# Attention with a quantized feed-forward block: reordering the first and last attention steps, rotated sums kept in PSUM, and a rotation table laid out by rows

## The chip, the cores and the metric

The kernel runs on one core of a Trainium2 chip. The metric is the device time of one execution in microseconds (us). Five engines work side by side, each through its own queue in order: TensorE (PE: matmuls and transposes, results into PSUM), VectorE (DVE), ScalarE (ACT), GpSimd (POOL) and SyncE (SP, which issues most of the DMA transfers here). Engines wait for each other through semaphores. [...] SBUF is the working memory.

## What is computed

One transformer layer, for 8 batches of 128 rows and 512 columns. The first half is a cross-attention with 32 query heads and 8 key/value heads of 128 columns, the second a gated feed-forward block whose weights are rounded to a table of 16 values (NF4) in blocks of 64. The reference, cut:

```python
def attention(query, key, value, mask, Wq, Wk, Wv, Wo):   # query = layernorm(x)
    q = apply_rope((query @ Wq).reshape(b, t, 32, 128))
    k = apply_rope((key @ Wk).reshape(b, t, 8, 128))
    v = (value @ Wv).reshape(b, t, 8, 128)
    logits = einsum('btkgd,bTkd->bkgtT', q, k) * ATTN_MULT
    logits = 30.0 * tanh(logits / 30.0)
    weights = softmax(where(mask, logits, -1e30))
    return einsum('bkgtT,bTkd->btkgd', weights, v).reshape(b, t, 4096) @ Wo

def apply_rope(x):      # x * cos + rotate_half(x) * sin
    ...

def ffn(x, w1, w2, w3):
    dq1, dq2, dq3 = nf4(w1), nf4(w2), nf4(w3)
    return (silu(x @ dq1.T) * (x @ dq2.T)) @ dq3.T

x = x + attention(layernorm(x), ctx, ctx, mask, Wq, Wk, Wv, Wo)
x = x + ffn(layernorm(x), w1, w2, w3)
```

## The kernel before

The order of every engine's work is written out by hand: the program is built in that order, each engine runs its own part of it as a queue, and no scheduler moves anything.

**Matrix products.** Each float32 operand is split in a high part (a copy to a narrower float, ScalarE, L155) and a low part (the difference, L156, VectorE or GpSimd). `product` (L165) does three matmuls for each pair of operands: high times low (L169), high times high (L170), low times high (L171).

**Stage 1, keys and values** (to about 106 us): the context is loaded in eight tiles, keys `pk` and values `pvp` are computed in tiles of 128 x 512 and written to DRAM. `loads` (L585) is the order of the loads on SP's queue: the first key weight, four context tiles, the table of rotations `tab`, two more key weights, and the rest. `rope` (L454) rotates a key or query tile: ScalarE copies the two halves of the PSUM tile, exchanged, into `rs` (L461, L462); VectorE multiplies the PSUM tile with the cosines into `rc` (L463); GpSimd multiplies `rs` with the signed sines (L464); and a sum of both goes to `kr` or `qr` (L465, on GpSimd unless an engine is named). `rc` and `rs` have two buffers each.

**Stage 2, attention** (to about 600 us): 64 steps `i` (the loop at L759), each for one batch and one key/value head with its four query heads. In step `i` stand, in this order: query tiles of the next half (`q_proj`, four in each group of four steps; the first group has them at steps 0, 0, 1 and 2), `project(i - 3)` (the output projection `po`, and the sum into `acc`, L702), `turn(i - 2)` (transposes `pt_a` and the split into `aT`), `values(i - 1)` (`pv`, and its division by the row sums into `ad`), and `scores(i)` (`pl`, then tanh and exp on ScalarE at L678 and L679, then the mask on GpSimd at L681). Query tiles `pq` and transposes `pt_a` share two PSUM banks with the tag `q`; `pl` has one bank (`s`), `po` one (`wo`). Near the end the sums of the second layer norm are taken from `acc` (`LayerNorm.sums`, L131: statistics at L133 and L134), its rows `xn_y` follow (L150), and their transposes `pt_y`, which use the banks `q`, `s` and `wo`.

**Dequantization** runs beside all that as a stream: one unit is a bound on ScalarE (`nm_w`, L195) and an accumulation on VectorE in PSUM (`nc_w`, L201), of 1024 columns in most tiles. `pump(n)` (L404) puts `n` units into the queues where it is called; `store` splits a finished tile, and for the first two weights writes it to DRAM. The last weight's tiles `w3t` stay in SBUF.

**Stage 3, feed-forward** (from about 603 us): `gate_up` for two halves and eleven tiles of hidden columns, then the down projection `pd` (from L865) with splits `hs` of the hidden values; the tiles `w3t` are dequantized while it begins, the last one (96 rows) only shortly before it is used.

Of the kernel before, what the change touches and what calls it, by code (L numbers as in the profile page):

```python
# [11 lines left out]
F32 = mybir.dt.float32  # L12
# [8 lines left out]
P = 128  # L21
B, T, D = 8, 128, 512
# [3 lines left out]
KT = D // P  # L26
# [19 lines left out]
def tables():  # L46
    e = np.arange(0, HD, 2, dtype=np.float32)
    inv = (np.float32(1.0) / np.float32(10000.0) ** (e / np.float32(HD))).astype(np.float32)
    phase = np.arange(T, dtype=np.float32)[:, None] * inv[None, :]
    phase = np.tile(phase, (1, 2)).T  # L50
    cos, sin = np.cos(phase).astype(np.float32), np.sin(phase).astype(np.float32)
    sgn = sin.copy()
    sgn[:HD // 2] *= -1


    bias = np.array([np.nextafter(BOUNDS[i], np.float32(np.inf)) if i in NEG else -BOUNDS[i]
                     for i in range(15)] + [0], dtype=np.float32) * np.float32(BIG)
    return (np.ascontiguousarray(np.stack([cos, sgn])),
            np.ascontiguousarray(np.broadcast_to(bias, (P, 16))))


# [1 line left out]
def block_kernel(ctx: ExitStack, tc: tile.TileContext, x, ctxt, mask, wq, wk, wv, wo, w1, w2, w3, w12t, w3_t,  # L63
                 rope_tab, nf_bias, out):
    nc = tc.nc
    V, S, Q, E = nc.vector, nc.scalar, nc.gpsimd, nc.tensor
# [4 lines left out]
    tp = ctx.enter_context(tc.tile_pool(name="tp", bufs=2))  # L71
# [20 lines left out]
    tab = cp.tile([P, 2, T], F32, name="tab")  # L92
# [69 lines left out]
            E.transpose(pt[:, k * P:(k + 1) * P], src[:, k * P:(k + 1) * P], ident)  # L162
        return lambda: split(hi, lo, pt.rearrange("p (k t) -> p k t", k=KT), V)

    def product(out, pairs, start=True, stop=True):  # L165

        n = len(pairs)
        for i, ((ah, al), (bh, bl)) in enumerate(pairs):
            E.matmul(out, ah, bl, start=start and i == 0, stop=False)  # L169
            E.matmul(out, ah, bh, start=False, stop=False)  # L170
            E.matmul(out, al, bh, start=False, stop=stop and i == n - 1)  # L171


    def scales(a, r, w):
# [115 lines left out]
    class Scales:  # L290
# [23 lines left out]
        def turn(self, tag):  # L314
            pt = bank(tag, f"pt_ar_{self.h}")[:2 * 16, :P]
            E.transpose(pt, self.s.rearrange("p t b -> p (t b)"), ident)

            def later():
                t = nf.tile([2 * 16, P], F32, tag="nf_st", name=f"art_{self.h}", bufs=1)
                S.copy(t, pt)  # L320
                nc.sync.dma_start(scale_d.rearrange("t j b h -> (t j b) h")[:, self.h * P:(self.h + 1) * P], t)
            stored.append(later)
# [81 lines left out]
    def pump(n):  # L404

        credit[0] += n
        while credit[0] > 0:
            credit[0] -= next(stream, n + credit[0])
# [17 lines left out]
    with ExitStack() as c1:  # L426

        xT = [wide(f"xT_{i}") for i in range(2)]
        cosq = a1.tile([P, T], F32, name="cosq")
        sgnq = a1.tile([P, T], F32, name="sgnq")  # L430
        mt = a1.tile([P, T], F32, name="mt")
        qr = {}
# [18 lines left out]
            t = wp.tile([P, 2, KT, HD], F32R, tag="wq", name=name, bufs=6)  # L451
            return t, lambda: split(t[:, 0], t[:, 1], raw, V if name == "wk_0" else Q)

        def rope(dst, src, cos, sgn, name, engine=None):  # L454

            hd = HD // 2
            every = lambda ap: ap.unsqueeze(1).to_broadcast([P, 4, T])
            src4 = src.rearrange("p (b t) -> p b t", t=T)
            c = tp.tile([P, 4, T], F32, tag="t1", name=f"rc_{name}")
            s = tp.tile([P, 4, T], F32, tag="t2", name=f"rs_{name}")  # L460
            S.copy(s[:hd], src4[hd:])  # L461
            S.copy(s[hd:], src4[:hd])  # L462
            V.tensor_tensor(c, src4, every(cos), ALU.mult)  # L463
            Q.tensor_tensor(s, s, every(sgn), ALU.mult)  # L464
            return lambda: (engine or Q).tensor_tensor(dst, c, s, ALU.add)  # L465
# [6 lines left out]
        def q_proj(u, g):  # L472
            kv, half = divmod(u, 2)
            if g == 0:
                qr[u] = a1.tile([P, 4, G, T], F32, tag="qr", name=f"qr_{u}", bufs=2)
            pq = bank("q", f"pq_{u}_{g}")
            w, t = wqt[kv, g], xT[half]
            product(pq, [((w[:, 0, k], w[:, 1, k]), (t[:, 0, k], t[:, 1, k])) for k in range(KT)])
            return lambda: rope(qr[u][:, :, g, :], pq, cosq, sgnq, f"q{u}_{g}", V if u < 1 else None)


        with ExitStack() as c3:
# [28 lines left out]
            def k_proj(kv, half):  # L511
                cols = slice(half * 512, half * 512 + 512)
                pk = bank("q", f"pk_{kv}_{half}")
                w = wkt[kv]
                product(pk, [((w[:, 0, k], w[:, 1, k]), (cT[0][:, k, cols], cT[1][:, k, cols])) for k in range(KT)])

                def later():
                    kr = kv1.tile([P, 512], F32, tag="kr", name=f"kr_{kv}_{half}")
                    add = rope(kr.rearrange("p (b t) -> p b t", t=T), pk, tab[:, 0], tab[:, 1], f"k{kv}_{half}",
                               V if kv < 3 else Q)  # L520

                    def last():
                        add()
                        nc.sync.dma_start(kr_d[kv, half], kr)
                    return last
                return later
# [51 lines left out]


            def load_tab(*_):  # L580
                nc.sync.dma_start(tab, rope_tab.rearrange("c d t -> d c t"))
                return lambda: None

            load = {"t": load_tab, "k": load_k, "c": load_c, "v": load_v, "q": load_first_q}
            loads = [(-1, "k", 0, 0)] + [(-1, "c", 0, k) for k in range(KT)]  # L585
            loads += [(-1, "t", 0, 0), (-1, "k", 1, 0), (0, "k", 2, 0), (0, "c", 1, 0), (0, "c", 1, 1), (1, "c", 1, 2), (1, "c", 1, 3)]
            loads += [(2, "v", 0, 0), (2, "v", 0, 1), (3, "v", 0, 2), (3, "v", 0, 3), (5, "k", 3, 0), (9, "k", 4, 0)]
            loads += [(12, "k", 5, 0), (15, "k", 6, 0), (17, "v", 1, 0), (18, "v", 1, 1), (19, "k", 7, 0)]
            loads += [(20, "v", 1, 2), (21, "v", 1, 3)] + [(24 + 2 * g, "q", g, 0) for g in range(G)]
# [82 lines left out]
        def scores(i):  # L672
            u, kv, b, bb = where(i)
            pl = bank("s", f"pl_{i}")
            E.matmul(pl, krt[kv, u % 2][:, bb * T:(bb + 1) * T], qr[u][:, bb].rearrange("p g t -> p (g t)"),  # L675
                     start=True, stop=True)
            th = at.tile([P, 512], F32, tag="th", name=f"th_{i}", bufs=3)
            S.activation(th, pl, AF.Tanh, scale=ATTN_MULT / CAP)  # L678
            S.activation(th, th, AF.Exp, scale=CAP)  # L679
            em[i] = th.rearrange("p (g t) -> p g t", g=G)  # L680
            Q.tensor_tensor(em[i], em[i], mt.unsqueeze(1).to_broadcast([P, G, T]), ALU.mult)  # L681
# [15 lines left out]
        def project(i):  # L697
            u, kv, b, bb = where(i)
            po = bank("wo", f"po_{i}")
            product(po, [((aT[i][:, 0, g], aT[i][:, 1, g]), (wot[kv, g][:, 0], wot[kv, g][:, 1]))  # L700
                         for g in range(G)])
            V.tensor_tensor(acc[b], acc[b], po, ALU.add)  # L702
# [46 lines left out]
                V.tensor_tensor(hT[half, h // 4][:, h % 4], sg, pu, ALU.mult)  # L749
            return later  # L750

        due = {0: [("o", 0, 0)], 1: [("o", 0, 1), ("o", 0, 2), ("o", 0, 3)]}
        xn = {}

        def turned(ks, tags):
# [3 lines left out]
        for i in range(N):  # L759
            u, kv, b, bb = where(i)  # L760
            s8 = i % 8
            if kv + 1 < NKV:
                if s8 == 0:
                    load_kv(kv + 1)
                if s8 < 4:
                    load_q(kv + 1, s8)
                else:
                    load_o(kv + 1, s8 - 4)
                due.setdefault(i + (2 if i < 4 else 1), []).append(("q" if s8 < 4 else "o", kv + 1, s8 % 4))
            tiles = {0: (0, 1), 1: (2,), 2: (3,), 3: ()}.get(i, (bb,)) if u + 1 < 2 * NKV else ()  # L770
            later = [q_proj(u + 1, g) for g in tiles]
            later = [f() for f in later]
            if i > 1:
                store()
                end_store()
            pump(1.5 if 2 < i < 58 else 1 if i in (0, 1, 58, 59) else 0)
            if 0 <= i - 3:
                project(i - 3)
            if i in (59, 61):
                ln = LayerNorm((i - 59, i - 58), f"y{i - 59}")  # L780
            if 59 <= i < 63:
                ln.sums(i - 59)
            if 0 <= i - 2:
                turn(i - 2)
            if 0 <= i - 1:
                values(i - 1)
            scores(i)
            if i == 61:
                xn.update({k: pair.rows(k, "xn") for k in (0, 1)})
            for f in later:  # L790
                f()
            pump(1.65 if 2 < i < 58 else 2 if i == 58 else 0)
            if i == 62:
                turned((0, 1), "qq")
            if i in (60, 62):
                ln.finish(Q)
                pair = ln
            for k in due.pop(i, ()):
                todo[k]()
            if i >= 61:  # L800
                load_w12(i - 61)

        project(N - 3)
        xn.update({k: pair.rows(k, "t2") for k in (2, 3)})
        turned((2,), "s")
        turn(N - 2)
        values(N - 1)
        turned((3,), "s")
        ln = LayerNorm((4, 5), "y1")
        ln.sums(4)  # L810
# [113 lines left out]
```

## Time and profile before

| what | us |
|---|---|
| median of three runs | 794.67 (794.63 to 794.92) |
| the profiled execution | 793.06 |
| its span, first to last instruction | 791.3 |
| TensorE busy | 777.4 (98% of the span) |
| VectorE busy | 626.9 (79%) |
| ScalarE busy | 586.0 (74%) |
| GpSimd busy | 472.6 (60%) |

The busy times are of the profiled execution. A matmul's end in the profile is modelled, and matmuls overlap, so the space between the starts of two matmuls tells more than the length of one. In a line of the timeline the first number is the start in us from the start of the span, the second the length; then engine, source line, operation, output and inputs, shape, how many were merged (x), and in brackets how long the engine stood idle before it and what ended that. In the waits view a line names the waiting engine, tile and line, what it waited for, then the sum in us, the number of waits and the longest.

### The profile page before, as it was taken

How to read it: one execution, taken by the hardware profiler on the slowest of the kernel's cores; microseconds unless marked ns; L12 is line 12 of the kernel's file. 1: busy time of each engine (PE TensorE's matmuls, PEld its weight loads, DVE VectorE, ACT ScalarE, POOL GpSimd, SP SyncE). 2: the span in 40 equal slices, each digit the busy share in tenths (PEclk: the TensorE clock that was granted, in tenths of full speed). 3: DMA queues.
4: the chain of work that ended last, by engine and by line, in shares of the span. 5: the costliest groups of instructions: out<-in, count | busy, mean ns of one | idle time of the engine just before them, and what ended most of it. 6: DMA issues, size and time to landing. Idle time of an engine off the chain costs nothing.

```text
span 791.3 us, 11200 instructions
## 1 busy us (share of the span) xinstructions
PE 777.4 (98%) x3737; PEld 628.3 (79%) x3737; DVE 626.9 (79%) x836; ACT 586.0 (74%) x821; POOL 472.6 (60%) x415
## 2 busy tenths in 40 slices
PE   8999997999999999999999999999999999999998
PEld 7788875778777878878787887878777888888887
DVE  6767677788888887888888878888876688888981
ACT  7458667889796978879797979898732587779740
POOL 3568448688787878777797877878652122232110
PEclk9999999999999999999999999999999999999999
DMA  6966735525337434517336432414133163651011
GB/s 229 297 190 198 213 107 174 147 80 173 90 120 206 136 104 121 173 55 227 94 109 191 133 92 94 138 57 128 58 104 107 49 173 98 186 160 47 11 53 54
DMA packets 73457, 102.44 MB, mean 129 GB/s; under 512 B 7832, under 2 KB 42968, under 8 KB 73400
## 3 DMA queue, kind: packets, MB, share of 16 engines
q1 hardware_dynamic: 70232, 90.19, 37.9%
q0 software_dynamic: 3168, 11.54, 4.6%
q8 instruction: 30, 0.49, 0.3%
q14 instruction: 27, 0.22, 0.1%
HBM read 79.32 MB, written 22.38 MB: 129 GB/s over the span
## 4 chain that ended last, share of the span: by engine, by line
PE 93%; ACT 2%; DVE 2%; issue 1%; DMA 1%; SPq 0%; POOL 0%; DVEq 0%; POOLq 0%; ACTq 0%
PE po L171 7%; PE po L170 7%; PE po L169 7%; PE pq L171 7%; PE pq L169 7%; PE pq L170 7%; PE pv L688 7%; PE pl L675 7%; PE pt_a L162 3%; PE pd L170 3%; PE pd L169 3%; PE pd L171 3%; PE pu L171 3%; PE pg L171 3%; PE pg L170 3%; PE pu L170 3%
## 5 line engine op out<-in xcount | busy, mean ns | idle before, releaser
L201 DVE SCALAR_TENSOR_TENSOR nc_w<-nm_w,nc_w 128x1024 f32<-128x1024 bf16 (+1 forms) x238 | 284.6, 1196 | 62.1 <-ACT nm_w L195 51.4
L195 ACT ACTIVATE nm_w<-w_w,bias 128x1024 bf16<-128x1024 f32 (+1 forms) x255 | 275.9, 1115 | 18.3 <-POOL w_w L205 8.7
L681 POOL TENSOR_TENSOR th<-th,mt 128x512 f32<-128x512 f32 x64 | 83.4, 1303 | 88.4 <-ACT th L679 81.5
L169 PE MATMUL pq<-xT,wq 128*128 128x512 f32 x256 | 123.9, 484 | 0.0
L169 PE MATMUL po<-wo,aT 128*128 128x512 f32 x256 | 102.1, 399 | 1.1 <-DVE acc L702 0.6
L171 PE MATMUL po<-wo,aT 128*128 128x512 f32 x256 | 100.5, 393 | 2.6 <-DVE aT L156 2.6
L171 PE MATMUL pq<-xT,wq 128*128 128x512 f32 x256 | 100.4, 392 | 0.0
L170 PE MATMUL pq<-xT,wq 128*128 128x512 f32 x256 | 100.1, 391 | 0.0
L170 PE MATMUL po<-wo,aT 128*128 128x512 f32 x256 | 100.0, 391 | 0.0
L464 POOL TENSOR_TENSOR rs_q<-rs_q,sgnq 128x512 f32<-128x512 f32 x64 | 83.0, 1296 | 13.0 <-ACT rs_q L462 12.9
L465 POOL TENSOR_TENSOR qr<-rc_q,rs_q 128x512 f32<-128x512 f32 x60 | 78.5, 1308 | 0.0
L678 ACT ACTIVATE th<-pl 128x512 f32<-128x512 f32 x64 | 38.3, 598 | 49.7 <-PE pl L675 48.4
L688 PE MATMUL pv<-vt,th 128*128 128x129 f32 x512 | 67.8, 275 | 1.3 <-POOL th L681 1.3
L169 PEld LDWEIGHTS pq<-xT,wq 128*128 128x128 f32 x256 | 48.2, 188 | 22.5 <-issue 10.8
L170 PEld LDWEIGHTS pq<-xT,wq 128*128 128x128 f32 x256 | 48.2, 188 | 22.3 <-issue 13.9
L675 PE MATMUL pl<-qr,krt 128*128 128x512 f32 x128 | 65.5, 593 | 0.0
L688 PEld LDWEIGHTS pv<-vt,th 128*128 128x128 f32 x512 | 62.2, 192 | 1.7 <-POOL th L681 1.7
L463 DVE TENSOR_TENSOR rc_q<-pq,cosq 128x512 f32<-128x512 f32 x64 | 44.0, 687 | 20.0 <-ACT rs_q L462 17.3
L205 POOL TENSOR_TENSOR w_w<-w_w,s_w 128x1024 f32<-128x1024 f32 (+1 forms) x17 | 39.6, 2327 | 33.1 <-DMA s_w<-scale_d 32.5
L171 PEld LDWEIGHTS po<-wo,aT 128*128 128x128 f32 x256 | 48.0, 188 | 14.1 <-DVE aT L156 3.8
L169 PEld LDWEIGHTS po<-wo,aT 128*128 128x128 f32 x256 | 48.1, 188 | 14.0 <-issue 2.1
L171 PEld LDWEIGHTS pq<-xT,wq 128*128 128x128 f32 x256 | 48.0, 188 | 10.7
(145 smaller groups left out, 1692.0 us busy)
## 6 DMA issues: line engine op xcount, KB each, us to landing
w12t_d<-dqt SPq DMA_DIRECT2D x22, 512.0 KB
w<-w12t_d POOLq DMA_DIRECT2D x22, 512.0 KB, 4.5
s_w<-scale_d SPq DMA_DIRECT2D x40, 256.0 KB
raw_wq<-in_L_xattn_Wq SPq DMA_DIRECT2D x32, 256.0 KB
raw_wo<-in_L_xattn_Wo SPq DMA_DIRECT2D x32, 256.0 KB
s_w<-scale_d SPq DMA_DIRECT2D x86, 64.0 KB
ws<-in_L_ffn_w SPq DMA_DIRECT2D x20, 256.0 KB
w_w<-in_w12t SPq DMA_DIRECT2D x10, 512.0 KB
```

The lines of the kernel that those rows point to most:

```text
L169: E.matmul(out, ah, bl, start=start and i == 0, stop=False)
L170: E.matmul(out, ah, bh, start=False, stop=False)
L171: E.matmul(out, al, bh, start=False, stop=stop and i == n - 1)
L195: S.activation(m, self.w, AF.Relu, bias=bias[:self.p, i:i + 1], scale=BIG if up else -BIG)
L201: V.scalar_tensor_tensor(self.c, m, step, self.c, ALU.min, ALU.subtract if i == POS[0] else ALU.add)
L205: Q.tensor_tensor(self.w, self.w, self.s, ALU.mult)
L463: V.tensor_tensor(c, src4, every(cos), ALU.mult)
L464: Q.tensor_tensor(s, s, every(sgn), ALU.mult)
L465: return lambda: (engine or Q).tensor_tensor(dst, c, s, ALU.add)
L675: E.matmul(pl, krt[kv, u % 2][:, bb * T:(bb + 1) * T], qr[u][:, bb].rearrange("p g t -> p (g t)"), start=True, stop=True)
L681: Q.tensor_tensor(em[i], em[i], mt.unsqueeze(1).to_broadcast([P, G, T]), ALU.mult)
L688: E.matmul(pv[:, g, :HD + 1], em[i][:, g], vt[kv][:, b], start=True, stop=True)
```

## The change

- The table of rotations is stored by partition, so that a partition's cosines and sines are one row of 1024 B; its load moves behind the second key weight.
- `product` can start with high times high. The first key tile does so.
- `rope` can leave the product with the cosines in the PSUM tile, in place of `rc`. The four query tiles of the second half (`u == 1`) do so, and their sums are made by VectorE, not GpSimd.
- In step 0, the copies of the second query tile come behind `scores(0)`; the two `pump(1)` of steps 0 and 1 move from the front of the step to its end. The `pump(1)` of step 59 goes away. `store` begins at step 4, not 2.
- Of the first output weights, two are split at the end of step 0 and two at the end of step 1 (before, one and three).
- In steps 59 to 62 the norm's sums come behind `turn`.
- Behind the loop, `turn(N - 2)` and `values(N - 1)` come ahead of the norm's rows 2 and 3 and their transposes.

```diff
-    return (np.ascontiguousarray(np.stack([cos, sgn])),
+    return (np.ascontiguousarray(np.stack([cos, sgn], axis=1)),
...
-    def product(out, pairs, start=True, stop=True):
+    def product(out, pairs, start=True, stop=True, high=False):
...
-            E.matmul(out, ah, bl, start=start and i == 0, stop=False)
-            E.matmul(out, ah, bh, start=False, stop=False)
-            E.matmul(out, al, bh, start=False, stop=stop and i == n - 1)
+            three = [(ah, bh), (al, bh), (ah, bl)] if high else [(ah, bl), (ah, bh), (al, bh)]
+            for j, (a, b) in enumerate(three):
+                E.matmul(out, a, b, start=start and i + j == 0, stop=stop and i == n - 1 and j == 2)
...
-        def rope(dst, src, cos, sgn, name, engine=None):
+        def rope(dst, src, cos, sgn, name, engine=None, apart=False):
...
-            c = tp.tile([P, 4, T], F32, tag="t1", name=f"rc_{name}")
+            c = src4 if engine is V and apart else tp.tile([P, 4, T], F32, tag="t1", name=f"rc_{name}")
...
-            return lambda: rope(qr[u][:, :, g, :], pq, cosq, sgnq, f"q{u}_{g}", V if u < 1 else None)
+            return lambda: rope(qr[u][:, :, g, :], pq, cosq, sgnq, f"q{u}_{g}", V if u < 2 else None, u == 1)
...
-                product(pk, [((w[:, 0, k], w[:, 1, k]), (cT[0][:, k, cols], cT[1][:, k, cols])) for k in range(KT)])
+                product(pk, [((w[:, 0, k], w[:, 1, k]), (cT[0][:, k, cols], cT[1][:, k, cols])) for k in range(KT)],
+                        high=(kv, half) == (0, 0))
...
-                nc.sync.dma_start(tab, rope_tab.rearrange("c d t -> d c t"))
+                nc.sync.dma_start(tab, rope_tab)
...
-            loads += [(-1, "t", 0, 0), (-1, "k", 1, 0), (0, "k", 2, 0), ...
+            loads += [(-1, "k", 1, 0), (-1, "t", 0, 0), (0, "k", 2, 0), ...
...
-        due = {0: [("o", 0, 0)], 1: [("o", 0, 1), ("o", 0, 2), ("o", 0, 3)]}
+        due = {0: [("o", 0, 0), ("o", 0, 1)], 1: [("o", 0, 2), ("o", 0, 3)]}
...
-            later = [f() for f in later]
-            if i > 1:
+            later = [f() for f in later[:1]] + later[1:]
+            if i > 3:
                 store()
                 end_store()
-            pump(1.5 if 2 < i < 58 else 1 if i in (0, 1, 58, 59) else 0)
+            pump(1.5 if 2 < i < 58 else 1 if i == 58 else 0)
             if 0 <= i - 3:
                 project(i - 3)
             if i in (59, 61):
                 ln = LayerNorm((i - 59, i - 58), f"y{i - 59}")
+            if 0 <= i - 2:
+                turn(i - 2)
             if 59 <= i < 63:
                 ln.sums(i - 59)
-            if 0 <= i - 2:
-                turn(i - 2)
             if 0 <= i - 1:
                 values(i - 1)
             scores(i)
+            later = later[:1] + [f() for f in later[1:]]
...
-            pump(1.65 if 2 < i < 58 else 2 if i == 58 else 0)
+            pump(1.65 if 2 < i < 58 else 2 if i == 58 else 1 if i < 2 else 0)
...
         project(N - 3)
+        turn(N - 2)
+        values(N - 1)
         xn.update({k: pair.rows(k, "t2") for k in (2, 3)})
         turned((2,), "s")
-        turn(N - 2)
-        values(N - 1)
         turned((3,), "s")
```

More of the change, by code (lines that the diff above doesn't have):

```diff
@@ L585, in block_kernel @@
             loads = [(-1, "k", 0, 0)] + [(-1, "c", 0, k) for k in range(KT)]
-            loads += [(-1, "t", 0, 0), (-1, "k", 1, 0), (0, "k", 2, 0), (0, "c", 1, 0), (0, "c", 1, 1), (1, "c", 1, 2), (1, "c", 1, 3)]
+            loads += [(-1, "k", 1, 0), (-1, "t", 0, 0), (0, "k", 2, 0), (0, "c", 1, 0), (0, "c", 1, 1), (1, "c", 1, 2), (1, "c", 1, 3)]
             loads += [(2, "v", 0, 0), (2, "v", 0, 1), (3, "v", 0, 2), (3, "v", 0, 3), (5, "k", 3, 0), (9, "k", 4, 0)]
```

## The prediction

> **What bounds the kernel now.** I read the page's chain of waits first, then TensorE's row of the waits view, then the timeline of single engines around every wait of TensorE that is longer than half a microsecond.
>
> ```profile
> PE 93%; ACT 2%; DVE 2%; issue 1%; DMA 1%; SPq 0%; POOL 0%; DVEq 0%; POOLq 0%; ACTq 0%
> ...
> PE po L171 <- DVE aT L156: 2.6, 2, 1.9
> PE pt_a L162 <- ACT wo L155: 1.4, 1, 1.4
> ...
> PE pt_y L162 <- DVE xn_y L150: 1.3, 1, 1.3
> PE pv L688 <- POOL th L681: 1.3, 1, 1.3
> ```
>
> TensorE carries 93% of the chain that ends last, and it waits rarely: no cause reaches 3 us in 791.3. So the change can only win or lose in a few places: the start (to 22.4 us, where the chain runs through DMA, ScalarE and VectorE), the first attention steps (118 to 137), the end of attention (568 to 600) and the last dequantized tile (761). Elsewhere matmuls of 512 columns start every 0.227 us, and other engines' work is hidden.
>
> ```profile
> 117.90 1.02 PE L675 MATMUL pl<-qr,krt 128*128 128x512 f32 x2
> ...
> 118.10 0.58 ACT L461 COPY rs_q<-pq 64x512 f32<-64x512 f32 x1 [1.75 <-PE pq L171]
> ...
> 120.36 0.58 ACT L678 ACTIVATE th<-pl 128x512 f32<-128x512 f32 x1
> ...
> 122.99 1.16 PE L688 MATMUL pv<-vt,th 128*128 128x129 f32 x8 [1.31 <-POOL th L681]
> ...
> 129.21 0.63 PE L162 MATMUL pt_a<-ident,ad 128*128 128x128 f32 x4 [1.44 <-ACT wo L155]
> ...
> 134.66 0.50 PE L171 MATMUL po<-wo,aT 128*128 128x512 f32 x1 [1.87 <-DVE aT L156]
> ```
>
> The first scores are there at about 118.8, but the tanh runs at 120.36, behind two copies and a bound (`nm_w`). TensorE's lost time up to 134.66, counted from the slot it was free in: 121.52 to 122.99, 127.61 to 129.21, 131.43 to 132.06 and 132.62 to 134.66, or 1.47 + 1.60 + 0.63 + 2.04 = 5.7 us.
>
> **Start.** The table's load moves behind the second key weight on SP's queue and is laid out in rows; the first tile starts with high times high. Today the first matmul is at 5.83, after the low half of the context (VectorE 5.08 to 5.77). The high half is done at 5.05, so it can start near 5.11: 0.72 us earlier. But matmuls are spaced 0.43 us until 10.26 and 0.227 after, so 0.72 us is 1.7 matmuls, 0.38 us later on. Even that isn't all won: the chain passes at 22.41 through key rotations on ScalarE and VectorE, which start with the context tile landing at 10.31. It has the same bytes queued ahead as before. [...] In the trace the small packets are mostly moved from 6.5 to 8 us, at 306 and 400 GB/s, but 5.5 to 6.5 dips to 221 and 188. [...] if the dip is the table's, about 0.5 us goes. I take 0.2 won, ends 0 and 0.6: the key weight's low half on POOL finishes earlier too (9.46 to 12.02 today), which unblocks VectorE's slow 1.59 us split at 10.98.
>
> **First attention steps.** In the changed order ScalarE does the first query's copies, tanh, exp, and only then the second query's copies. Tanh starts at 118.79 (0.89 after `pl`, as at 146.28 to 147.17), exp 119.42, POOL's mask (1.26) 120.12 to 121.38. So the 1.47 us wait for the mask goes. **But a new wait takes its place.** The rotated product now stays in the PSUM tile, so a `q` bank comes free only after the final add. There are two `q` banks. The third query tile needs the first's; its add stands on VectorE behind the second's cosine product, which needs the second's copies, now behind exp:
> - copies start 119.96 (exp + 0.54) and 120.55, done 121.13; cosine product 121.16; the add 121.76 (VectorE's spacing of such pairs is 0.60), done 122.44.
> - The third tile starts at 122.50; its slot today is 118.76. New stall 3.74 us. Everything behind it on TensorE waits too.
>
> From there: twelve matmuls (0.34 + 11 x 0.227) to 125.33; values 0.89, scores 0.86, to 127.08; the fourth tile to 129.81 with no wait (its bank's add is done near 123.4, on VectorE instead of 1.3 us each on POOL); transposes 0.44 to 130.25 (the normalized values `ad` are done at 128.2); values and scores to 132.00. ScalarE: third copies end 126.7, tanh 127.11, exp, bound, two weight casts to 130.45, fourth copies to 131.6, cast of `aT` to 132.2. VectorE: the two weight splits that today take 1.48 each beside POOL (4.43 for three from 128.98) find POOL idle and take 0.69, until 131.8; product, then low half of `aT` at 132.4 to 133.08. So the projection starts 132.25 and its third matmul is at 133.13, against 134.66. Lost 3.74 + 0.1 + 0.25 + 0.4 in place of 5.7: **1.5 us won**. The ends: the in-place product has no row; nearest is the accumulation `nc_w` held in PSUM, 1.20 for 1024 columns, so 0.69 for 512 as now; at 1.28 (an add beside POOL) the stall grows by 0.6 twice. If VectorE meets POOL as today, another 0.7. So 0 to 2.2 won. The store moved to later steps and SP's weight-scratch store passing two weight loads cost nothing: TensorE doesn't need them for several steps of 7.68 us; POOL loses four adds (5.2 us).
>
> **End of attention.**
>
> ```profile
> 571.40 0.47 PE L169 MATMUL po<-wo,aT 128*128 128x512 f32 x1 [0.61 <-DVE acc L702]
> ...
> 572.83 0.50 PE L171 MATMUL po<-wo,aT 128*128 128x512 f32 x1 [0.73 <-DVE aT L156]
> ...
> 597.45 0.63 PE L162 MATMUL pt_y<-ident,xn_y 128*128 128x128 f32 x4 [1.33 <-DVE xn_y L150]
> ```
>
> - One dequantization unit leaves step 59 (ScalarE 1.15 at 568.26, VectorE 1.23 at 569.43), and the statistics (0.71 + 0.18) go behind the split. Today VectorE adds at 570.57 and splits at 572.12. Then it adds at 568.64 and splits at 569.68 to 570.34, before TensorE is free at 570.63. The third matmul comes at 571.09, not 572.83: **1.74 us won**. In steps 60 to 62 the swap gains nothing; no wait stands there.
> - The last transposes and values of attention now go before the norm's transposes `pt_y`. Today: `pt_y` at 597.45, `pt_a`, values, second `pt_y` at 599.48 (same bank, so it waits 2.03 for the first's evacuation, 1.34 of it filled), projection at 599.89. Then: `pt_a` 595.97, values wait for the mask until 596.90 (POOL 595.54 to 596.84), end 597.79. VectorE holds `rows` behind this step's split (597.2), reciprocal and division (598.1 to 598.8), so `xn_y` starts 598.83 and `pt_y` 599.52 (0.69 later, as today). The second follows 2.03 later at 601.55 with nothing between; projection 601.96. **2.07 us lost**; ends 1.4 and 2.4.
>
> **The unit taken out is done later.** From step 59 on the dequantization runs one unit late, and at the end that shows.
>
> ```profile
> 757.86 0.69 DVE L237 TENSOR_TENSOR w_w<-nc_w,s_w 96x512 f32<-96x512 f32 x1
> ...
> 759.76 1.57 POOL L156 TENSOR_TENSOR w3t<-w_w,w3t 96x512 fp32r<-96x512 f32 x1 [7.40 <-ACT w3t L155]
> ...
> 761.47 0.41 PE L169 MATMUL pd<-w3t,hs 96*128 96x512 f32 x1
> ```
>
> The last weight tile is ready at 761.33, TensorE takes it at 761.47: no slack. VectorE is full from 728 to 759, and in the changed order it has one 1024-column unit (1.23) and one `hs` split (0.47) more before `w_w`: 1.70 late. One of two splits that POOL slows to 1.64 (746.73) would slide past POOL's work and give 0.95 back. So 0.75 to 1.70; I take 1.0 lost.
>
> **Sum:** -0.2 - 1.5 - 1.74 + 2.07 + 1.0 = about -0.4 us. The profiled execution took 793.06 (span 791.3 and 1.76 around it), so 792.7 for one like it; that execution is 1.61 below the median 794.67, and the median goes to **794.2**. Within 0.2% (1.6 us) a measurement of this kernel can't tell it from no change.
>
> **Rivals.**
> - *Clock falls (slower).* The largest gap of TensorE in this region today is about 2.0 us, and matmuls after it are still 0.23 apart. [...] The new stall is 3.74[...]. By the row it costs nothing more[...]. With 2.4: 796.6. [...] I take the row. With the upper ends of the other costs, this case gets 24%.
> - *Handover costs nothing (faster).* If `rows` doesn't come late, or the last weight tile keeps up, 2 us more are won: 792.2. For it: POOL and VectorE are less in each other's way. Against: the orders are fixed. 18%.
> - *The start wins as much as TensorE could* (0.4 to 0.6): 793.8, inside the forecast.
>
> The forecast's case gets 58%. The range 792.4 to 796.8 takes in the faster case's near side and the clock's.
>
> **What would show it.** First tanh near 118.8; third query tile waiting for VectorE's `qr` about 3.7 us, then spacing 0.227 (0.43 would be the clock); the third `po` matmul about 1.5 earlier; no wait at step 59; `pt_y` waiting about 1.7 and again 1.6; and `pd` waiting for `w3t` about 1 us. It is wrong if the third tile's wait is gone, or if matmuls slow down.

## The result, and the profile after

| what | before | changed |
|---|---|---|
| median, 8 runs each, taken together (us) | 794.49 (793.90 to 794.92) | 796.30 (795.38 to 797.83) |
| ratio | 1 | 1.0026 [1.0015, 1.0037] |
| profiled execution (us) | 793.06 | 795.38 |
| its span (us) | 791.3 | 793.6 |
| mean granted clock of TensorE in it | 1.000 | 0.996 |

The changed kernel is slower by 0.26%. In the changed kernel source lines stand one to four further down, and the three matmuls of `product` are one line, L172. The page's chain of waits, which before ran along TensorE for the whole execution, now breaks off at the last dequantized tile, so it explains only the end:

```profile
PE 3%; issue 2%; POOL 0%; DVE 0%; POOLq 0%; ACT 0%
```

The waits view of TensorE shows the rest. The long waits of `po` and `pt_a` and the 1.3 us for the mask are gone (0.3 us of `po` are left); in their place stand one long wait of the third query tile, two of `pt_y` and a short one of `pd`:

```profile
PE pq L172 <- DVE qr L467: 4.0, 1, 4.0
PE pt_y L162 <- DVE xn_y L150: 1.5, 1, 1.5
PE pt_y L162 <- DVE xT L156: 1.4, 1, 1.4
...
PE pd L172 <- POOL w3t L156: 0.4, 1, 0.4
```

The timeline of the first attention steps in the changed kernel:

```profile
117.20 1.02 PE L678 MATMUL pl<-qr,krt 128*128 128x512 f32 x2
118.26 0.60 ACT L681 ACTIVATE th<-pl 128x512 f32<-128x512 f32 x1 [2.64 <-PE pl L678]
...
120.75 0.70 DVE L465 TENSOR_TENSOR pq<-pq,cosq 128x512 f32<-128x512 f32 x1 [4.39 <-ACT rs_q L464]
121.35 1.46 DVE L467 TENSOR_TENSOR qr<-pq,rs_q 128x512 f32<-128x512 f32 x2
...
122.18 4.58 PE L172 MATMUL pq<-xT,wq 128*128 128x512 f32 x12 [3.96 <-DVE qr L467]
...
126.61 1.05 PE L691 MATMUL pv<-vt,th 128*128 128x129 f32 x8
```

Tanh starts 2.1 us earlier than before (1.4 us when counted from the first scores), as meant. The first query tile's sum (the first of the two at 121.35) stands behind the second tile's cosine product, and the third tile waits 3.96 us for it. Then comes what the sum of the prediction left out: twelve matmuls last from 122.18 to 126.61, 4.43 us, where at full clock they take 2.85 (122.80 to 125.65 in the run with useless matmuls below). The view by stretches gives the granted clock. A line has the stretch, its length, then for each engine the busy time in it and the number of instructions; PEclk, third from the end, is the granted share of TensorE's full clock:

```profile
core 0: us, PE busy (x) PEld busy (x) DVE busy (x) ACT busy (x) POOL busy (x), PEclk, DMA share, GB/s
118.80:122.20 3.40, 0.02 (x1) 0.05 (x1) 1.36 (x3) 3.31 (x6) 2.49 (x2) 1.00 0.97 320
122.20:125.60 3.40, 3.40 (x8) 2.72 (x9) 2.95 (x4) 0.72 (x2) 0.00 (x0) 0.50 0.01 2
125.60:129.00 3.40, 3.40 (x18) 2.61 (x18) 0.96 (x3) 1.60 (x3) 0.95 (x1) 1.00 0.74 200
596.60:600.00 3.40, 1.00 (x7) 0.77 (x8) 2.09 (x4) 0.58 (x1) 0.00 (x0) 1.00 0.98 352
600.00:603.40 3.40, 3.40 (x11) 2.72 (x10) 2.23 (x5) 0.58 (x1) 0.00 (x0) 0.51 0.00 0
```

For 3.4 us behind the wait TensorE runs at half its clock. The same happens at 600 us, where no wait is long: the stretch ahead holds the two waits of `pt_y`, with a few values and transposes beside them, and TensorE is busy for 1.00 of 3.40 us. Such a stretch at half clock is called a fall below. One lowers the mean clock of an execution by 0.002 (half of 3.4 us in 793), so a mean of 0.996 stands for two. The timeline of TensorE there:

```profile
594.98 1.16 PE L691 MATMUL pv<-vt,th 128*128 128x129 f32 x8 [0.37 <-POOL th L684]
597.60 0.66 PE L162 MATMUL pt_y<-ident,xn_y 128*128 128x128 f32 x4 [1.46 <-DVE xn_y L150]
599.66 0.78 PE L162 MATMUL pt_y<-ident,xn_y 128*128 128x128 f32 x4 [1.40 <-DVE xT L156]
600.09 4.57 PE L172 MATMUL po<-wo,aT 128*128 128x512 f32 x12
```

The last w3 tile is late by less than I took:

```profile
760.24 0.68 DVE L238 TENSOR_TENSOR w_w<-nc_w,s_w 96x512 f32<-96x512 f32 x1
...
762.14 1.55 POOL L156 TENSOR_TENSOR w3t<-w_w,w3t 96x512 fp32r<-96x512 f32 x1 [9.27 <-ACT w3t L155]
...
763.75 0.96 PE L172 MATMUL pd<-w3t,hs 96*128 96x512 f32 x3 [0.37 <-POOL w3t L156]
```

**Theory 1:** TensorE's clock falls to half for 3.4 us behind the new waits; each fall costs up to half of that, 1.7 us, on top of the wait. **Theory 2, the rival:** the waits alone cost the time, and the clock is immaterial.

### The profile page after: what moved, and what is told of

Read it like the earlier page. It is cut to its first block, busy times and chain, and to the rows that moved or that the text cites. A ratio compares the mean times of both kernels' runs of the same rounds, so it can differ in the third digit from the quotient of the medians.

```text
span 793.6 us, 11197 instructions
## 1 busy us (share of the span) xinstructions
PE 779.5 (98%) x3737; PEld 629.6 (79%) x3737; DVE 624.8 (79%) x840; ACT 586.2 (74%) x821; POOL 466.1 (59%) x411
## 5 line engine op out<-in xcount | busy, mean ns | idle before, releaser
L172 PE MATMUL pq<-xT,wq 128*128 128x512 f32 x768 | 211.0, 424 | 4.0 <-DVE qr L467 4.0
L172 PEld LDWEIGHTS pq<-xT,wq 128*128 128x128 f32 x768 | 145.2, 190 | 60.1 <-issue 24.1
L172 PE MATMUL po<-wo,aT 128*128 128x512 f32 x768 | 190.3, 397 | 0.4 <-ACT aT L155 0.3
L172 PEld LDWEIGHTS po<-wo,aT 128*128 128x128 f32 x768 | 144.3, 189 | 34.8 <-issue 1.9
L172 PE MATMUL pg<-xT,w 128*128 128x512 f32 x264 | 63.7, 390 | 0.0
L172 PE MATMUL pu<-xT,w 128*128 128x512 f32 x264 | 63.5, 389 | 0.0
L172 PE MATMUL pd<-w3t,hs 128*128 128x512 f32 (+3 forms) x297 | 60.8, 366 | 0.4 <-POOL w3t L156 0.4
L172 PEld LDWEIGHTS pd<-w3t,hs 128*128 128x128 f32 (+1 forms) x297 | 51.3, 189 | 9.9 <-POOL w3t L156 0.8
L172 PEld LDWEIGHTS pu<-xT,w 128*128 128x128 f32 x264 | 49.5, 188 | 10.3
L172 PEld LDWEIGHTS pg<-xT,w 128*128 128x128 f32 x264 | 49.3, 188 | 10.1
L155 ACT CAST aT<-pt_a 128x512 fp32r<-128x512 f32 x64 | 36.6, 571 | 27.6 <-PE pt_a L162 27.6
```

The lines of the kernel that those rows point to most:

```text
L155: S.copy(hi, src)
L172: E.matmul(out, a, b, start=start and i + j == 0, stop=stop and i == n - 1 and j == 2)
```

## The experiments

All ran on one chip, in three groups, each with its own runs of the kernel before: 16, 26 and 38 of them, with medians of 794.86, 794.61 and 794.36 us. Ratios are to these, with a 95% interval; they differ from the quotient of the medians by up to 0.0006.

### The tail's order, undone and alone

`e1_tail_back` (from the changed kernel) and `e2_tail_only` (from the kernel before) make the same edit in opposite directions:

```diff
         project(N - 3)
-        turn(N - 2)
-        values(N - 1)
         xn.update({k: pair.rows(k, "t2") for k in (2, 3)})
         turned((2,), "s")
+        turn(N - 2)
+        values(N - 1)
```

> The changed kernel with one edit undone: behind the last attention step the last product's transposes (pt_a of tile 62) and values (pv of tile 63) stand again behind the rows and turns of y2 and y3 (pt_y), as before. Changed kernel: 796.3 us. Theory 1 (TensorE's clock fell to half for about 3.4 us twice, once at the third query tile's wait and once behind the two waits of pt_y; each fall costs about 1.7 us): both the two pt_y waits (2.0 us) and their clock fall (1.7 us) go, so about 792.6 us, and the profile shows a granted clock of 0.5 only near 122 us. Theory 2 (the waits alone cost the time, the clock is immaterial): 794.3 us.

> The kernel before with the tail edit alone: pt_a of tile 62 and pv of tile 63 ahead of the rows and turns of y2 and y3. Kernel before: 794.5 us. Theory 1 (two pt_y waits of 1.4 to 1.5 us each, net 2.0 us, and behind them half a clock for 3.4 us, 1.7 us): 798.2 us, with granted clock about 0.5 for one stretch of 3.4 us behind the second pt_y. Theory 2 (the waits alone): 796.5 us, clock at 1.0 throughout.

Undone: **792.72 us**, ratio to before 0.9971 [0.9960, 0.9983]. Alone: **798.37 us**, 1.0045 [1.0031, 1.0059]. One edit, some 3.6 us each way: theory 1's 792.6 and 798.2, not theory 2's 794.3 and 796.5. With the edit alone, the profile has two stretches at half clock, one behind the other:

```profile
597.50:600.90 3.40, 1.58 (x12) 1.15 (x11) 2.48 (x5) 0.35 (x2) 0.76 (x2) 1.00 1.10 396
600.90:604.30 3.40, 2.37 (x8) 2.08 (x9) 1.29 (x2) 0.84 (x2) 0.00 (x0) 0.50 0.35 128
604.30:607.70 3.40, 3.40 (x10) 2.63 (x9) 1.64 (x5) 0.00 (x0) 0.00 (x0) 0.50 0.00 0
```

The fall began earlier within the tail here, so the second `pt_y` wait lies in the first stretch at half clock; with 2.37 us busy at half clock, TensorE stayed at half clock for one stretch more. Theory 1 had counted one stretch here, on top of the usual time of the kernel before, which holds a fall in the first steps (shown below). This profile has none there and two in the tail, so 798.2 was met by another count. With the edit undone, only the fall near 123 us is left in the profile.

### Keeping TensorE busy in the same waits

These two leave all waits of other engines where they are and give TensorE useless work in its own.

```diff
+            if i == 1:
+                fill("pv", "f0", 15)          # 30 in the run with transposes
             later = [q_proj(u + 1, g) for g in tiles]
...
+        f1_ = fill("q", "f1", 5)              # 10
         turned((2,), "s")
+        fill("q", "f2", 5, f1_)               # 10
         turned((3,), "s")
```

> The changed kernel with useless matmuls where TensorE would wait: 15 ahead of the third query tile, 5 ahead of the turn of y2 and 5 between the turns of y2 and y3; nothing reads their results. Each is near 0.23 us, so they lie within the waits of 4.0, 1.5 and 1.4 us. Theory 1 (the falls of the clock come from TensorE's idle time): the granted clock stays at 1.0 through both places, 796.3 less two falls of 1.7 us, about 792.9 us. Theory 2 (waits alone): 796.3 us or a little more.

> As the run with useless matmuls, but with useless transposes of the identity (30, 10 and 10 of them, about 0.1 us each) in the same three places; nothing reads their results. Theory 1, in the form that transposes do not hold the clock up (the clock fell behind the turns of y2 and y3 although eight transposes stood between the waits): the clock falls to half as in the changed kernel, 796.3 us. If transposes count as work for the clock: about 792.9 us. Theory 2 (waits alone): 796.3 us with or without falls of the clock.

With matmuls **793.05 us**, 0.9980 [0.9971, 0.9990]; with transposes **792.90 us**, 0.9973 [0.9962, 0.9984]. More work in the queue makes the changed kernel some 3.3 us faster: theory 2 falls. My own guess on transposes falls too: they keep the clock up as matmuls do. The same stretch of the first steps in the two runs, matmuls first:

```profile
118.80:122.20 3.40, 3.40 (x16) 2.51 (x14) 0.83 (x2) 3.23 (x5) 1.99 (x2) 1.00 1.07 369
122.20:125.60 3.40, 2.87 (x13) 2.35 (x13) 3.26 (x5) 1.34 (x3) 0.57 (x1) 1.00 0.14 38
```

```profile
118.80:122.20 3.40, 2.83 (x26) 2.59 (x24) 1.29 (x2) 3.31 (x6) 2.47 (x2) 1.00 0.86 283
```

So the transposes of `pt_y` and the values beside them had simply been too little: 1.00 us of work in 3.4.

A third run takes away the useless matmuls between the two `pt_y` only, so that one of the tail's two waits stays:

```diff
-        f1_ = fill("q", "f1", 5)
+        fill("q", "f1", 5)
         turned((2,), "s")
-        fill("q", "f2", 5, f1_)
         turned((3,), "s")
```

> As the run with useless matmuls, but without the 5 between the turns of y2 and y3, so that of the tail's two waits the second, 1.4 us, stays; nothing reads the useless results. In the profiles so far every stretch of 3.4 us ahead of a fall has TensorE busy for at most 1.6 us, and those of 2.1 us or more at full clock were followed by none. Theory 1 as it now stands (the share of idle time in one stretch of 3.4 us counts, so a wait of 1.4 us and small ones beside it, 1.7 us in all, are at or under the bound): 793.2 us in most runs, as with both waits filled, some runs 1.6 us above. Theory 2 of the tail (one wait of 1.4 us behind a few transposes is enough): a fall in every run, about 794.7 us.

**793.26 us** (0.9992 [0.9985, 0.9999]): 13 of 16 runs had a mean clock of 1.000 and three 0.998 (794.5 to 795.2). Here one wait of 1.4 us is mostly harmless; two of them, 2 us apart, are not. Its profile:

```profile
598.66 0.66 PE L162 MATMUL pt_y<-ident,xn_y 128*128 128x128 f32 x4 [1.40 <-DVE xT L156]
599.07 3.02 PE L172 MATMUL po<-wo,aT 128*128 128x512 f32 x12
```

### The kernel before, once more

Its runs scatter in two heaps, and the profile that I predicted from lay in the lower one, 1.6 us under the median.

> The kernel before, unchanged. In the runs with the first four experiments 13 of its 16 runs had a mean granted clock of 0.998 and 793.7 to 795.7 us, 2 had 1.000 and 793.3 and 793.8 us; its first profile (793.06 us) had 1.000. Theory 1: the usual run holds one fall of the clock of about 1.6 us that the first profile did not show, so 794.7 us with half a clock for some 3.4 us in one place, most likely behind the waits of 1.4, 0.5 and 1.9 us between 127.6 and 134.7 us that the changed kernel no longer has, or else behind the tail's pt_y wait of 1.3 us near 597 us. Theory 2 (clock immaterial): no stretch at half clock, and the spread has another cause.

The median was 793.62 us: six of the ten runs had a clock of 1.000 (793.06 to 793.80 us), four 0.998 or 0.997 (794.58 to 795.19). The profiled run (794.8 us, clock 0.998) has a fall, and in the first place named:

```profile
132.15 0.50 PE L169 MATMUL po<-wo,aT 128*128 128x512 f32 x1 [0.47 <-ACT aT L155]
132.48 0.40 PE L170 MATMUL po<-wo,aT 128*128 128x512 f32 x1
134.74 0.50 PE L171 MATMUL po<-wo,aT 128*128 128x512 f32 x1 [1.86 <-DVE aT L156]
...
136.07 0.63 PE L169 MATMUL po<-wo,aT 128*128 128x512 f32 x1
136.50 0.63 PE L170 MATMUL po<-wo,aT 128*128 128x512 f32 x1
```

From 135.4 on the matmuls stand 0.43 us apart. The view by stretches of the same profile:

```profile
132.00:135.40 3.40, 1.39 (x5) 0.87 (x6) 3.37 (x5) 3.37 (x7) 3.40 (x3) 1.00 1.01 277
135.40:138.80 3.40, 3.40 (x10) 2.52 (x9) 2.47 (x3) 0.98 (x1) 3.40 (x4) 0.50 0.52 205
```

These are the waits of the first profile to within 0.02 us, but there the matmuls behind 134.66 stood 0.23 us apart and the granted clock over these two stretches was 1.00. What differs is where the stretches of 3.4 us begin. In the trace of the changed kernel the granted clock changes at 122.18, 125.59, 600.05 and 603.46 us: 3.41 us apart within a fall, and 140 times 3.413 us from one fall to the other. In `e6_no_first` the two falls begin at 135.29 and 599.50 us, 136 times 3.413 us apart, in `e7_add_first` at 130.59 and 598.21, 137 times. So I took the edges of all stretches of an execution to follow from one change. In the first profile the one change stands at 791.92 us, behind the last instruction; 193 times 3.413 us ahead of it a stretch begins at 133.15 and takes in more of the busy time behind the wait:

```profile
133.15:136.56 3.41, 1.90 (x8) 1.58 (x9) 3.37 (x6) 3.14 (x5) 3.41 (x3) 1.00 1.03 282
```

Seven profiles of this study have these waits. In the four with a fall (here, and in `e6_no_first`, `e10_start_only` and `e12_step59_unit` below) the stretch ended at 134.0 to 135.4 us, with 1.40 to 1.60 us busy; in the three without (the first one, `e2_tail_only` and `e11_step59_only`) it ended at 136.4 to 136.7, with 1.90, 1.57 and 2.0 us busy. Only the 1.57 does not fit a bound between the two.

Of the 38 runs of the kernel before in the last group, 12 had a clock of 1.000 and a median of 793.1 us, 26 a lower one and 794.6. So the usual run of before holds one fall, of 1.5 us; the changed kernel's eight runs had clocks of 0.996 to 0.991, two falls or more. (The heaps overlap a little: the mean clock also counts the end of an execution, where TensorE is done, as `e8_best` shows below.)

### The first attention steps, undone and mended

`e6_no_first` takes these steps back to the kernel before (the copies' place, the sums on GpSimd into `rc`, `due`, `store`, `pump`), and keeps the rest of the change.

```diff
-            return lambda: rope(..., V if u < 2 else None, u == 1)
+            return lambda: rope(..., V if u < 1 else None)
...
-            later = [f() for f in later[:1]] + later[1:]
+            later = [f() for f in later]
```

> The changed kernel with the edit of the first attention steps undone (tanh behind the copies, sums on GpSimd into another buffer, one wo split due in step 0, units as before); start, step 59 and tail as changed. By the traces the first steps lost 0.6 us in the changed kernel's profile, with one fall of the clock in it. Theory 1: 796.3 less 0.6 to 1.0 if the usual run of before holds no fall in these steps (795.5 us); 796.3 plus up to 1.0 (797 us) if its usual fall lies there. Theory 2 (the 4.0 us wait against the waits that go, no clock): the edit alone saves about 1.0 us, so 797.3 us.

**796.78 us**, 1.0029 [1.0017, 1.0042]: nearest to theory 1's upper case (797), but its six runs reach from 795.47 to 797.82, and theory 2's 797.3 lies among them, so its time tells nothing apart. Its profile has the falls of theory 1: one from 135.3 us, as in the kernel before, and two stretches in the tail.

`e7_add_first` keeps the change and emits the first query tile's sum ahead of the second tile's copies:

```diff
             scores(i)
-            later = later[:1] + [f() for f in later[1:]]
...
-            for f in later:
-                f()
+            for k, f in enumerate(later):
+                (f() if k else f)()
```

> The changed kernel with the first query tile's sum emitted right behind the first scores, ahead of the second tile's copies and products, so that its bank comes free near 117.8 us and not at 122.1. Theory 1: the wait of 4.0 us goes and with it this fall of the clock; about 3.4 us of wait and 1.6 us of clock, of which a later wait for the splits of wo or for the second tile's bank may take 1 to 2 back: 796.3 less 3 to 5, about 792.3 us. Theory 2 (waits alone): 796.3 less 1.5 to 3, about 794 us.

**794.53 us** (792.21 to 795.53), 1.0000 [0.9991, 1.0010]: a miss by 2.2 us, nearer theory 2's number. The waits view of its profile says what failed:

```profile
PE pt_a L162 <- DVE qr L467: 2.4, 1, 2.4
```

The third tile no longer waits, but the first transposes do, for the bank of the third query tile, whose sum on VectorE (128.61 to 129.29) stands behind two splits of output weights. With that, the clock falls here as well, 8.4 us later than in the changed kernel (the view by stretches of the same profile):

```profile
127.20:130.60 3.40, 1.16 (x11) 1.19 (x12) 3.37 (x7) 2.93 (x6) 2.07 (x2) 1.00 0.55 173
130.60:134.00 3.40, 3.40 (x9) 1.90 (x8) 3.37 (x6) 1.13 (x3) 0.42 (x1) 0.50 0.69 180
```

From the first `pl` to the transposes `pt_a` of step 3 it takes 17.9 us with a fall, where the changed kernel takes 19.77 with one. So these steps win 1.9 us, where I had counted on 4: a wait of 2.4 us took the place of the one of 4.0, and the fall stayed. It costs little here, though. In the profile of `e8_best` below the same steps have the same wait of 2.5 us and no fall, and take 17.63 us: TensorE is faster there and then waits 1.1 us for `aT` from VectorE, which `e7_add_first` does not. The tail's fall, from 598.2 us, is still there too, as expected.

### Start and step 59, each alone on the kernel before

`e10_start_only` has the diff's lines for the table, `loads` and `high`. `e11_step59_only`:

```diff
-            pump(1.5 if 2 < i < 58 else 1 if i in (0, 1, 58, 59) else 0)
+            pump(1.5 if 2 < i < 58 else 1 if i in (0, 1, 58) else 0)
...
-            if 59 <= i < 63:
-                ln.sums(i - 59)
             if 0 <= i - 2:
                 turn(i - 2)
+            if 59 <= i < 63:
+                ln.sums(i - 59)
```

and `e12_step59_unit` gives the missing unit back in the feed-forward part:

```diff
-        pump((3.45 if n < last - 3 else 2.6) if n > 0 else 0)
+        pump((3.45 if n < last - 3 else 2.6) if n > 0 else 1)
```

> The kernel before with the edits of the start alone (rotation table by rows, loaded behind the second key tile, the first product with its high halves first). The profile of the changed kernel against that of before had the first pl 0.7 us earlier; over all profiles of this study it is 0.3 us earlier on average, and the prediction took 0.2. Start worth 0.7: 793.9 us; worth 0.2 to 0.3: 794.3 us; both with the usual fall of the clock as in before (794.6 us).

> The kernel before with the edit of step 59 alone (no unit of the planner in step 59, LayerNorm sums behind the turn). By the traces the step wins 1.9 us and the last w3t tile, a unit late, gives 0.4 back: 794.6 less 1.5, about 793.1 us. By the prediction's terms, 1.74 less 1.0: 793.9 us.

> As the run before this, with one unit more of the planner in the first step of the feed-forward part, so that the last w3t tile is not late. If the missing unit is what makes it late: 0.4 us under the run before this by the traces (1.0 by the prediction's term), about 792.7 us, and no wait of pd for w3t in the profile. If the feed-forward part has no room for a unit at that place: as the run before this or slower.

The start alone: **794.23 us**, 0.9997 [0.9989, 1.0006], so 0.1 us by the medians, and not told from nothing; the 0.7 us between the first two profiles was mostly scatter of the start. Step 59 alone: **791.68 us**, 0.9968 [0.9955, 0.9980]. Its five runs all had a clock of 1.000; against the runs of before with that clock (793.1) it wins 1.4 us, as the traces said. In the profiled run the stretches of the clock lie as in the first profile of before (one ends near 136.4 us); why none of the other four fell, though their first steps have the waits of before, stays open. With the unit given back: **792.60 us**, 0.9975 [0.9966, 0.9984], over 15 runs with mixed clocks. In its profile `pd` no longer waits for `w3t`, and the feed-forward part takes 188.35 us in place of 188.77, so the missing unit is what made the tile late; but the time is unclear: the seven runs with a clock of 0.999 or more have a median of 791.4, 0.3 us under the run without the unit, less than either scatters.

### A version ahead of both

`e8_best` is the changed kernel with the edits of `e7_add_first`, the tail's order of before, and the unit of `e12_step59_unit`.

> The changed kernel with the sum emitted early as in the run before this, the tail's order as in the kernel before, and one unit more of the w3 planner ahead in the first step of the feed-forward part, in place of the one taken from step 59. Theory 1: 796.3 less 4 (first steps), less 3.6 (tail), less 0.4 (last w3t tile): about 788.5 us, granted clock 1.0. Theory 2: 796.3 less 2.3, 2.0 and 0.4: about 791.6 us.

**789.69 us** (789.00 to 790.36), 0.9941 [0.9929, 0.9954]: between the two theories and nearer the first. By the profiles the first steps win 2.1 us against the changed kernel (not 4), the tail 3.7 and the feed-forward part 0.6, which makes 789.9. In its profile no fall is left while TensorE works. The mean clock of its profile (0.999) is lowered by the last 3.2 us, in which only the final sum and the store run (the view by stretches):

```profile
782.00:785.20 3.20, 3.18 (x27) 2.97 (x25) 0.00 (x0) 0.00 (x0) 0.00 (x0) 1.00 0.12 41
785.20:788.40 3.20, 0.00 (x0) 0.00 (x0) 0.42 (x1) 0.00 (x0) 0.00 (x0) 0.78 0.12 41
```

An order without the wait of 2.5 us for `qr` wasn't tried.

## Why the prediction was wrong

The forecast was 794.2 us and no change; it was 796.3 and slower. The profiles of the two runs with both waits filled have no fall, so they give the terms without the clock, cut at the first `pl`, the first `pt_a` of step 3, the first `pl` of step 63 and the first `pg`.

| term | predicted | without falls | in the changed kernel's profile |
|---|---|---|---|
| start | -0.2 | -0.25 (mean of 9 profiles against 5, each scattering over 0.7 to 1.2) | -0.70 |
| first attention steps | -1.5 | 18.2 against 19.19: -1.0 | 19.77: +0.58 |
| step 59 | -1.74 | 453.5 against 455.27: -1.75 | 453.44: -1.83 |
| tail | +2.07 | 12.86 against 10.74: +2.1 | 14.44: +3.70 |
| last w3 tile | +1.0 | 188.8 against 188.2: +0.6 | 188.77: +0.60 |
| sum | -0.4 | -0.3 | +2.35 |

- **The sum held, the clock was left out of it.** The two places at which the last two columns differ most, by 1.57 us each, are the two falls: 3.1 us of the profile. This closes: 793.1 for before without a fall, less 0.3, plus 3.1 is 795.9, and the five runs of the changed kernel with a clock of 0.996 have a median of 795.96. The matmuls behind the third tile's wait stand 0.43 us apart at first, which the prediction had named as the sign of the clock.
- **The step that failed is "I take the row"** in the rival of the falling clock. The row was one execution, in which a gap of 2.0 us was followed by matmuls 0.23 us apart; the new wait is twice as long, and in another execution of the same kernel even the old gap is followed by 3.4 us at half clock. The stretches of 3.413 us begin at another place in the two traces: the one around the old gap ended at 136.56 us in the first, with 1.90 us busy and no fall behind it, and at 135.41 in the second, with 1.40 us and a fall. So one profile can't clear a gap.
- **The rival itself was too narrow.** It looked at the one stall of 3.74 us alone, and its 2.4 us were an estimate of mine; the fall behind that wait cost 1.57 us in the trace. The tail's fall came from two waits of 1.46 and 1.40 us; it stood in none of my cases. With its two waits it is what undoing the tail's order gives back, 3.6 us. That the rival's 796.6 lies near the measured 796.3 is luck: it left out the tail's fall, and kept one of before that goes.
- **"That execution is 1.61 below the median"** was carried over as a constant. It was a fall of the clock that the usual run has and the profiled one had not. The change takes away the waits behind which it stood (`po` now starts after 0.28 us of idle time) and makes others: constant it was not.
- **First steps:** the wait was 3.96 us (3.74 predicted), in the place and for the cause named. The term was 0.5 us too large, most of it in the third tile's start, 4.98 us behind the first scores and not 4.60; with the fall the steps lose.
- **Step 59 and the tail without its fall** came as worked out. **The last tile:** `w_w` came at 760.24, 2.4 us after 757.86, in an execution 1.75 us behind by then (`pg` began at 604.85, not 603.10), and `pd` waits 0.37 us; the term was 0.4 us too large, and the 0.6 measured lies under its own low end of 0.75.
- **The table's rows:** a gain from them was an estimate, from the dip to 221 and 188 GB/s at 5.5 to 6.5 us; the run of the start alone (794.23 us against 794.36) doesn't show one.

## What to carry to other kernels

Price a new wait of TensorE together with its neighbours: add up the idle time in any 3.4 us around it. In these runs the stretches of 3.41 us ahead of a fall held 1.79 to 3.41 us of it, and a fall cost 0.3 us (`e7_add_first`, first steps, where TensorE would soon have waited anyway) to 1.6 us (changed kernel). When the profiled execution is faster than the median, look at its mean granted clock before using its gaps as proof of anything. And when an order of work is changed to end a wait, follow the bank or buffer to its next taker, since that is where the wait turned up again here (2.4 us at the first transposes, `e7_add_first`).

## What the runs showed of the hardware

- **Share, not length.** The fourteen profiles have eleven falls. Cut at the clock's own edges in the traces, the stretch of 3.41 us ahead of them had TensorE busy for 0.00 to 1.62 us (0.00 and 1.05 in the changed kernel, 0.75 in `e1_tail_back`, 1.16 and 1.21 in `e7_add_first`, 1.62 in `e2_tail_only`, 1.40 in the kernel before). In six profiles (the first one, the changed kernel, `e1_tail_back`, `e2_tail_only`, `e5_before_again`, `e7_add_first`) some 1330 more stretches at full clock lie between 10 to 13 us and 777 us. One of them held so little (1.57, in `e2_tail_only`); the rest held 1.90 or more, and no fall followed them. So in these profiles, by modelled busy time and but for that one, the two kinds part between 1.6 and 1.9 of 3.4 us. An unbroken gap wasn't needed: the waits of 1.46 and 1.40 us in the changed kernel's tail stood with 1.05 us of work in their stretch.
- **At half clock more was needed:** stretches with 2.01 and 2.35 us busy (`e6_no_first`, `e2_tail_only`) were followed by another at half clock, those with 2.75 or more by full clock (2.77 at 598.2 us in `e7_add_first`, 2.90 in `e10_start_only`, 2.94 in `e12_step59_unit`).
- **Transposes count** for keeping the clock: with 2.83 us of PE work, nearly all of it useless transposes, at 118.80 to 122.20 the clock stayed full (`e4_fill_transposes`), where it fell with 0.02 us (changed kernel); and the two fills end within 0.15 us of each other (793.05 and 792.90).
- **A product left in PSUM cost nothing more:** in the changed kernel's profile the four cosine products into the PSUM tile took 0.70 us each, those into SBUF 0.69 in the mean; VectorE's sum that reads it there took 0.68, as the fastest from SBUF. Its price is the bank, held until the sum: the third query tile waited 3.96 us for it.
